# A two-layer graph network on one core: score weights loaded first by column halves, score products split in two sums

## The chip, the cores and the metric

The kernel runs on one NeuronCore of one Trainium2 chip. The metric is the device time of one execution in microseconds (us). A core has five engines with instruction queues of their own: TensorE (PE; its weight loads are listed as PEld), VectorE (DVE), ScalarE (ACT), GpSimd (POOL) and SyncE (SP), which here only issues DMAs. ACT and POOL issue DMAs too. All DMAs share 16 DMA engines.

## The reference

128 graphs of 128 nodes with 512 features pass through two layers, all in float32.

```python
# layer 0
h = maximum(layernorm(x), 0)
Xw = h @ Wv + bv;  sj = Xw @ aw[:512];  si = Xw @ aw[512:]
e = leaky_relu(sj[:, None, :] + si[:, :, None] + ab, 0.2)
T = adj * exp(e);  T = T / (sum(T, -1) + 1e-12)
H = h @ Wk[0] + (T @ h) @ Wk[1] + (T @ T @ h) @ Wk[2] + biases
x = x + relu(H)
# layer 1
h = maximum(layernorm(x), 0)
q, k = split(h @ Wqk);  v = h @ Wv1
w = mask * sum(q * (adj @ (k * mask)), -1) / sqrt(512)
x = x + softmax(w over nodes) * v
```

Two rearrangements matter here. Layer 0 needs from Wv only two columns, Wv times each half of `aw`; they are put beside Wk[2], so one product gives h @ Wk[2] and both attention terms. Layer 1 needs from Wqk only the 512 x 512 matrix Wq Wk^T, the score matrix: q . (adj k) = h Wq Wk^T (adj h)^T. It is computed once, from Wqk transposed.

## The kernel before, in words

**Pairs.** Layer 0 takes the graphs in 64 pairs p (`G` = 2). Each 512 x 512 product of a pair is one level of Strassen (`strassen`): seven products in the order 1, 5, 6, 2, 7, 3, 4 on four PSUM banks, the partial sums moved between the banks by ACT copies. `y2(p)` is h @ Wk[2] with the two attention columns, on the banks of set2 (a2, b2, c2, e2). `y10(p)` is h @ Wk[1] and h @ Wk[0] side by side, on set1 (a1, b1, c1, e1), into which `seed_a` and `seed_e` first copy the biases. Left operands are the transposed h and four sums of its blocks (`left_sums`). Right operands are blocks of the weights and four differences of them (`combine`): `right2` for y2, `right10` for y10. `attention(p)` makes T from the two columns, the adjacency and an exponential. For that, `spread_columns` transposes the column over the partitions; for pairs 0 and 1 this is done on TensorE in the middle of y10(0)'s first product or behind y2(1). `inner` and `outer` apply T, and `norm2` makes h for layer 1, which follows from about 1300 us on with its own loop.

**Before pair 0's y2** stands the set-up, which the change rewrites. All line numbers are those of the kernel before.
- Loads (lines 144 to 190). SP issues x of pair 0, wqk in four chunks of 128 rows (`wqk_sb`, named tl in the profile), x of pair 1, and then the weights of layer 0 by `rows` (170 to 174): wv0 (t), Wk[2] (w) and Wk[1], Wk[0] (r). `rows` permutes the rows so that chunk c goes to partitions 32c to 32c + 31, four rows to each. The chunks 0 and 1 go on SP, 2 and 3 on POOL, there behind a one-element copy (`gate`, L178) that reads wqk's third chunk.
- `weights_transposed(c)` transposes chunk c of wqk on TensorE in groups of four, and ACT and VectorE copy them out of PSUM into `wqt` and `wkt`. Filling products on ones (`warm`, `warm_whole`) stand between the chunks.
- `score_matrix(f)` (L316 to L323) then makes 128 rows of the score matrix with four accumulated products on a bank of set1; ACT copies it to `rl`.
- Pair 0's h is normalised from `statistics` and transposed on TensorE (`transposed_by_pe`); later pairs go by a store to DRAM and four reloads in blocks (`by_blocks`: hd, hv), which VectorE transposes (`transposed`, in `begin`).
- `attention_columns` (L252 to L262) makes the two columns Wv aw on VectorE: eight products of 128 x 512 with a sum each (L258), and two small copies into the weights of y2 (w).
- `constant_columns` and `attention_constant` give the constant bv . aw + ab, which a small TensorE product in y2(0), behind its seventh product, adds up over the partitions; VectorE copies it to `cz`.

**What sets the order.** A scheduler orders each engine's instructions by its own estimate of when each will be ready. `tc.issue_after(x)` forbids it to put an instruction before x on its engine. `ordered` (L88 to L91) chains all TensorE work in the order of the program. `behind(what, op)` (L83 to L86) puts an operation behind the latest one recorded under a name: "wk" and "wq" for the set-up's copies on VectorE and ACT, "u" for the attention columns, "u2", "s7" for copies inside a Strassen product, "rs" and "aggr" for statistics, "right" for weight differences, "lrelu" and "t" for the attention. These helpers record all their operations at one line, so in the profile most TensorE work is L91, and many copies are L86: tiles tell them apart. A DMA queue takes its issues in program order, each also waiting until the DMA that used its semaphore eight issues earlier has landed.

## Time and profile before

| | |
|---|---|
| Time, median of 3 runs | 2207.72 us (2206.92 to 2208.58) |
| The profiled execution's own time | 2207.71 us |
| Its span, first to last instruction | 2205.9 us |
| TensorE busy | 2197.3 us of it |
| First score product | at 13.19 us |
| First product of y2(0) | at 28.27 us |
| First product of y2(1) | at 49.37 us |

Times of the profile count from the start of the span. A row of the timeline gives start, duration, engine, line, operation, output tile <- input tiles, shape and count, and in brackets how long the engine stood idle before it, and what ended this. A float32 product is two instructions in the profile, whose modelled ends overlap those that follow, so distances are taken from start to start. In the chain of waits each row is a start, a duration and what the chain was in: an engine's work, a DMA under way, or "issue", for which the profile shows no cause.

### The profile page before, as it was taken

The page shows a single profiled execution, that of the slowest core. Times are in us where ns is not written, and L with a number is a line of the kernel's source. Part 1 is how long each engine was busy: PE and PEld are TensorE (multiplying, and loading weights), DVE is VectorE, ACT ScalarE, POOL GpSimd, SP SyncE. Part 2 cuts the span into 40 slices and gives each one's busy share as a digit, 9 for nine tenths or more (in the row PEclk, how much of TensorE's full clock was granted, in tenths as well). Part 3 has the DMA queues.
Part 4 walks back from the last instruction along what each step waited for, and adds up shares of the span by engine and source line. Part 5 has one row for each costly group of instructions (what it writes and reads, how often), then busy time and mean ns, then how long its engine had stood idle before and what let it go on. Part 6 is the DMA issues. An engine that isn't in the chain of part 4 may idle for free.

```text
span 2205.9 us, 29564 instructions
## 1 busy us (share of the span) xinstructions
PE 2197.3 (100%) x8127; PEld 1536.1 (70%) x8127; DVE 1699.8 (77%) x4544; ACT 1233.0 (56%) x2854; POOL 782.6 (35%) x957
## 2 busy tenths in 40 slices
PE   9999999999999999999999999999999999999998
PEld 6666666665666666566666666688788878887886
DVE  6778788777878877777877777588777777777777
ACT  4555555555555455555545554456666666666665
POOL 3222222222222222222222222255545554555454
PEclk9999999999999999999999999999999999999999
DMA  7788788887878888887878887867888788787877
GB/s 212 204 226 241 221 237 241 234 245 226 247 223 244 234 239 234 225 245 225 243 222 239 232 232 207 285 180 220 234 226 228 214 236 224 231 212 230 233 212 182
DMA packets 431874, 503.14 MB, mean 228 GB/s; under 512 B 102113, under 2 KB 280289, under 8 KB 427741
## 3 DMA queue, kind: packets, MB, share of 16 engines
q1 hardware_dynamic: 379544, 374.67, 56.1%
q0 software_dynamic: 51744, 126.05, 23.2%
q8 instruction: 65, 1.06, 0.2%
q14 instruction: 101, 0.82, 0.1%
q10 hardware_dynamic: 420, 0.54, 0.1%
HBM read 287.17 MB, written 213.94 MB: 227 GB/s over the span
## 4 chain that ended last, share of the span: by engine, by line
PE 98%; DMA 1%; DVE 1%; issue 0%; SPq 0%; DVEq 0%; POOL 0%
PE a L91 29%; PE c L91 26%; PE b L91 26%; PE e L91 17%; DMA t<-in_L_gnn_Wv_dram 0%; DMA tl<-in_L_gnn_Wqk_dram 0%; DVE junk L258 0%; DVE c L720 0%; DVE h L720 0%; DVE junk L720 0%; SPq L146 0%; DVEq L1429 0%; DVE x L389 0%; PE a L194 0%; SPq L101 0%
## 5 line engine op out<-in xcount | busy, mean ns | idle before, releaser
L720 POOL TENSOR_TENSOR c<-s,c 128x512 f32<-128x512 f32 (+1 forms) x186 | 201.2, 1095 | 252.3 <-DVE s L720 247.2
L475 POOL DMA_DIRECT2D fd<-fw x124 | 78.8, 639 | 492.8 <-DVE fw L463 458.5
L111 POOL DMA_DIRECT2D agb<-in_adj_dram x256 | 149.9, 592 | 260.2 <-DVE aT L86 235.5
L91 PE MATMUL a<-r,x 128*128 128x512 f32 x512 | 240.7, 592 | 0.0
L91 PE MATMUL b<-rw,in 128*128 128x256 f32 x884 | 212.0, 379 | 0.0
L91 PEld LDWEIGHTS b<-rw,in 128*128 128x128 f32 x884 | 168.0, 190 | 23.3 <-issue 0.5
L91 PEld LDWEIGHTS a<-r,x 128*128 128x128 f32 x512 | 97.1, 190 | 95.0 <-issue 91.3
L86 ACT COPY s<-c 128x257 f32<-128x257 f32 (+1 forms) x128 | 61.6, 481 | 171.4 <-PE c L91 171.4
L86 ACT COPY b<-a 128x257 f32<-128x257 f32 (+1 forms) x128 | 59.4, 464 | 167.7 <-PE a L91 165.2
L720 POOL TENSOR_TENSOR c<-c 128x1024 f32<-128x1024 f32 x61 | 144.2, 2363 | 10.9 <-DVE c L720 10.4
L91 PE MATMUL a<-w,x 128*128 128x257 f32 x512 | 132.0, 380 | 1.2 <-DVE w L86 1.1
L91 PE MATMUL b<-w,sx 128*128 128x257 f32 x512 | 132.1, 380 | 0.1
L463 DVE STREAM_TRANSPOSE fw<-hv 128x256 f32<-128x256 f32 x248 | 88.3, 414 | 52.1 <-DMA hv<-h2d 51.7
L91 PE MATMUL c<-t,sx 128*128 128x512 f32 x256 | 120.3, 592 | 0.0
L91 PE MATMUL e<-t,sx 128*128 128x512 f32 x256 | 120.3, 592 | 0.0
L91 PE MATMUL c<-t,x 128*128 128x512 f32 x256 | 120.3, 592 | 0.0
L91 PE MATMUL b<-t,sx 128*128 128x512 f32 x256 | 120.3, 592 | 0.0
L91 PE MATMUL b<-r,sx 128*128 128x512 f32 x256 | 120.3, 592 | 0.0
L720 DVE SCALAR_TENSOR_TENSOR junk<-agg,wscale,c 128x512 f32<-128x512 f32 x126 | 96.2, 763 | 30.0 <-POOL c L720 24.8
L720 ACT ACTIVATE c<-c,wcol 128x512 f32<-128x512 f32 x124 | 86.3, 720 | 55.7 <-DVE wcol L720 55.7
L86 ACT COPY c<-b 128x257 f32<-128x257 f32 (+1 forms) x128 | 59.4, 464 | 98.9 <-PE b L91 98.9
L91 PEld LDWEIGHTS a<-w,x 128*128 128x128 f32 x512 | 97.1, 190 | 15.9 <-DVE w L86 1.9
(282 smaller groups left out, 5318.3 us busy)
## 6 DMA issues: line engine op xcount, KB each, us to landing
fd<-fw POOLq DMA_DIRECT2D x93, 512.0 KB, 4.8
xg<-in_x_dram SPq DMA_DIRECT2D x64, 512.0 KB, 7.0
x1d<-x SPq DMA_DIRECT2D x64, 512.0 KB, 5.6
h2d<-h SPq DMA_DIRECT2D x64, 512.0 KB, 3.0
hd<-h SPq DMA_DIRECT2D x63, 512.0 KB, 3.1
hv<-hd SPq DMA_DIRECT2D x252, 128.0 KB, 3.9
hv<-h2d SPq DMA_DIRECT2D x248, 128.0 KB, 4.4
h<-h2d SPq DMA_DIRECT2D x62, 512.0 KB, 7.7
```

Of the source, the lines that this page charges most:

```text
L86: return op(*args, **how)
L91: done["mm"] = op(*args, **how).ins
L111: nc.gpsimd.dma_start(agb[p][c * S32:(c + 1) * S32].rearrange("p g q i -> p (g q) i"), v[c])
L463: done["c12"] = nc.vector.transpose(blocks[:, k, j].rearrange("p f (n b) -> p f n b", n=Q), hv[:, j].rearrange("p n (k f a) -> p k f n a", ...
L475: done["fd"] = nc.gpsimd.dma_start(FD[q].rearrange("p o j k n -> p o (j k n)")[:, slots], FW[0].rearrange("p o j k n -> p o (j k n)")[:, s ...
L720: done[engine] = op(*args, **how).ins
```

## The change

- wqk is loaded first, before x of pair 0, in eight DMAs: by column halves (`oh`: the first or second 256 columns of Wq and of Wk at once), and in each by 128-row chunks. Each partition gets two pieces of 1 KB.
- `rows` splits by f in place of c: each DMA fills all 128 partitions with one row of 2 KB each.
- wv0 and Wk[2] are loaded wholly on SP, x of pair 1 between the two; the gate of POOL's loads reads the last of wv0, and POOL keeps half of Wk[1] and Wk[0]. The adjacency loads of pairs 0 and 1 stand behind these.
- The transposes run by quarters (`ch`, `oh`), and each score product is two sums: over the first 256 columns of Wq and Wk, then over the rest, added to the same bank. The program alternates transposes and score products, and pair 0's transposes stand between score products too.
- Of the filling products, one small one and two whole banks stay, all at the start.
- VectorE: pair 0's statistics stand behind the first transposed copies; pair 1's statistics and normalisation move from before y2(0) into it; two of the four differences of `right10` run beside y2(0), one behind `lrelu`, one behind `t`; the left sums come behind the attention columns. Both copies of pair 0's transposes are on ACT.

The diff, cut to its core:

```diff
+    for oh in range(2):
+        for ch in range(2):
+            part = [bass.AP(tensor=wqk.tensor, offset=wqk.offset + (ch * HC + c) * P * 2 * D + oh * HD,
+                            ap=[[2 * D, P], [D, 2], [1, HD]]) for c in range(HC)]
+            for c in range(HC):
+                nc.sync.dma_start(wqk_sb[:, ch * HC + c].rearrange("p (a o) -> p a o", a=2)[:, :, oh * HD:(oh + 1) * HD],
+                                  part[c])
     load_x(0)
-    for c in range(DC):
-        nc.sync.dma_start(wqk_sb[:, c], wqk[c * P:(c + 1) * P])
-    load_x(1)
...
-        for c in chunks:
-            queue.dma_start(dst[c * S32:(c + 1) * S32],
-                              w[c * P:(c + 1) * P].rearrange("(f a) o -> a f o", a=S32))
+        for f in chunks:
+            queue.dma_start(dst[:, f], bass.AP(tensor=w.tensor, offset=w.offset + f * S32 * D,
+                                               ap=[[P * D, DC], [D, S32], [1, D]]))
...
-    done["gate"] = nc.gpsimd.tensor_copy(gate, wqk_sb[:, 2, :1]).ins
+    for dst, w in weights0[:2]:
+        rows(dst, w)
+        if dst is wv0_sb:
+            load_x(1)
+    done["gate"] = nc.gpsimd.tensor_copy(gate, wv0_sb[:, DC - 1, :1]).ins
...
+    def weights_transposed(ch, oh, banks):
+
+        for a, bank in enumerate(banks):
+            pt = bank.rearrange("p (k n) -> p k n", n=P)
+            for c in range(HC):
+                for o in range(HC):
+                    at = a * D + (oh * HC + o) * P
+                    ordered(nc.tensor.transpose, pt[:, o * HC + c if a else c * HC + o, :],
+                            wqk_sb[:, ch * HC + c, at:at + P], ident)
...
-    def score_matrix(f):
+    def score_matrix(f, oh):
         bank = set1[f]
-        for o in range(DC):
+        for o in range(oh * HC, (oh + 1) * HC):
             ordered(nc.tensor.matmul, bank, wqt[:, o, f].rearrange("p c a -> p (c a)"), wkt[:, o],
-                    start=(o == 0), stop=(o == DC - 1))
+                    start=(o == 0), stop=(o == DC - 1), skip_group_check=True)
...
-            (nc.vector.tensor_copy if j else nc.scalar.copy)(dst[:, j], pt)
+            nc.scalar.copy(dst[:, j], pt)
...
+    warm(1, e2)
+    warm_whole(b2)
+    warm_whole(c2)
+    done["warm"] = done["wk"] = done["wq"] = done["mm"]
+    weights_transposed(0, 0, (a2, e2))
+    weights_transposed(1, 0, (c1, e1))
+    attention_vector_columns()
+    attention_vector(0)
+    weights_transposed(0, 1, (a2, e2))
+    attention_vector(1)
+    score_matrix(0, 0)
+    masks()
+    score_matrix(1, 0)
+    h0_rs = behind("wk", statistics, xg[0], "wq")
+    behind("aggr", bias_columns)
+    weights_transposed(1, 1, (a2, e2))
+    score_matrix(2, 0)
+    score_matrix(3, 0)
+    h0 = behind("wq", norm_relu, xg[0], True, h0_rs)
+    done["wq"] = done["h"]
+    score_matrix(0, 1)
     hT0 = lefts.tile([P, G, DC, N], FP, name="x")
+    transposed_by_pe(h0, hT0, (a2, e2))
+    behind("wk", behind, "rs", attention_columns)
+    LEFT[0] = behind("u", left_sums, hT0)
+    for f in range(1, Q):
+        score_matrix(f, 1)
     for p in range(2):
+        behind("loads", load_adj, p)
     with tc.issue_after(done["u"]):
         right2 = combine(halves(r2, W2), [t2[:, i] for i in range(4)])
+    def beside_y2():
+        RS0[1] = behind("right", statistics, xg[1], "u2")
+        bias()
+        constant_columns()
+    right10_steps = combine_steps(halves(r10, HD), pairs(t10))
+    right10 = combined(halves(r10, HD), pairs(t10))
+    with tc.issue_after(done["m"]):
+        y2(0, {2: beside_y2, 7: attention_constant})
+        with tc.issue_after(done["right"]), tc.issue_after(done["rs"]):
+            for step in right10_steps[:2]:
+                step()
+        behind("u2", seed_a)
+        behind("s7", norm0, 1, RS0.pop(1))
+        behind("s7", seed_e)
         spread_columns(0)
         attention(0)
+        behind("lrelu", right10_steps[2])
+        behind("t", right10_steps[3])
```

More of the change, by code (lines that the diff above doesn't have):

```diff
@@ L170, in rows @@
     def rows(dst, w, chunks=range(DC), queue=nc.sync):
-        for c in chunks:
-            queue.dma_start(dst[c * S32:(c + 1) * S32],
-                              w[c * P:(c + 1) * P].rearrange("(f a) o -> a f o", a=S32))
+        for f in chunks:
+            queue.dma_start(dst[:, f], bass.AP(tensor=w.tensor, offset=w.offset + f * S32 * D,
+                                               ap=[[P * D, DC], [D, S32], [1, D]]))
     gate = setup.tile([P, 1], FP, name="gate")
-    done["gate"] = nc.gpsimd.tensor_copy(gate, wqk_sb[:, 2, :1]).ins
     weights0 = [(wv0_sb, wv0), (r2[:, :, 1:1 + D], wk[2])] + [(r10[:, :, k], wk[1 - k]) for k in range(2)]
+    for dst, w in weights0[:2]:
[3 more added lines that the diff above has]
+    done["gate"] = nc.gpsimd.tensor_copy(gate, wv0_sb[:, DC - 1, :1]).ins
     with tc.issue_after(done["gate"]):
-        for dst, w in weights0[:2]:
+        for dst, w in weights0[2:]:
             rows(dst, w, range(HC, DC), nc.gpsimd)
@@ L184 @@
         nc.gpsimd.dma_start(awc, aw.rearrange("(a p c) o -> p a (c o)", a=2, c=DC))
-        nc.gpsimd.dma_start(ab_bc, bcast(ab, 0, 1))
-        for dst, w in weights0[2:]:
-            rows(dst, w, range(HC, DC), nc.gpsimd)
-    for dst, w in weights0:
+        done["loads"] = nc.gpsimd.dma_start(ab_bc, bcast(ab, 0, 1)).ins
+    for dst, w in weights0[2:]:
         rows(dst, w, range(HC))
@@ L298, in bias @@
         for i, to in enumerate((bias_a, bias_e)):
-            behind("wk", over_partitions, to[:, 1], bkt[:, 0, i * n:(i + 1) * n], n)
-    def weights_transposed(chunks):
-        banks = [a2, e2, a1, b1, c1, e1]
-        for c in chunks:
-            for a in range(2):
-                bank = banks[(c * 2 + a) % len(banks)]
-                pt = bank.rearrange("p (o i) -> p o i", o=DC)
-                for o in range(DC):
-                    at = a * D + o * P
-                    ordered(nc.tensor.transpose, pt[:, o, :], wqk_sb[:, c, at:at + P], ident)
-                if a:
-                    done["wk"] = behind("wq" if c == HC else "wk", nc.scalar.copy if c == HC else nc.vector.tensor_copy, wkt[:, :, c * P:(c + 1) * P], pt).ins
-                else:
-                    done["wq"] = behind("wq", nc.scalar.copy, wqt[:, :, :, c, :], pt.rearrange("p o (f a) -> p o f a", f=Q)).ins
@@ L316, in score_matrix @@
-    def score_matrix(f):
+            behind("aggr", over_partitions, to[:, 1], bkt[:, 0, i * n:(i + 1) * n], n)
+    def weights_transposed(ch, oh, banks):
[6 more added lines that the diff above has]
+                            wqk_sb[:, ch * HC + c, at:at + P], ident)
+            if a:
+                on = "wq" if oh > ch else "wk"
+                done[on] = behind(on, nc.scalar.copy if oh > ch else nc.vector.tensor_copy,
+                                    wkt[:, oh * HC:(oh + 1) * HC, ch * HD:(ch + 1) * HD],
+                                    bank.rearrange("p (o n) -> p o n", o=HC)).ins
+            else:
+                done["wq"] = behind("wq", nc.scalar.copy,
+                                    wqt[:, oh * HC:(oh + 1) * HC].rearrange("p o f c a -> p (o f) c a")[
+                                        :, :, ch * HC:(ch + 1) * HC],
+                                    bank.rearrange("p (c o a) -> p o c a", c=HC, a=S32)).ins
@@ L318, in score_matrix @@
+    def score_matrix(f, oh):
         bank = set1[f]
-        for o in range(DC):
+        for o in range(oh * HC, (oh + 1) * HC):
             ordered(nc.tensor.matmul, bank, wqt[:, o, f].rearrange("p c a -> p (c a)"), wkt[:, o],
-                    start=(o == 0), stop=(o == DC - 1))
+                    start=(o == 0), stop=(o == DC - 1), skip_group_check=True)
         done["m"] = done["mm"]
-        nc.scalar.copy(rl[:, f, 0], bank)
+        if oh:
+            done["wq"] = behind("wq", nc.scalar.copy, rl[:, f, 0], bank).ins
@@ L759, in inner_sums @@
                 lambda: dve(nc.vector.tensor_sub, s[:, 3], b[0, 1], s[:, 1])]
-    warm(7, e2)
+    warm(1, e2)
     warm_whole(b2)
-    done["warm"] = done["mm"]
-    h0_rs = statistics(xg[0])
-    done["wk"], done["wq"] = done["rs"], done["ln"]
-    weights_transposed(range(1))
+    warm_whole(c2)
[5 more added lines that the diff above has]
+    weights_transposed(0, 1, (a2, e2))
@@ L768 @@
+    attention_vector(1)
[7 more added lines that the diff above has]
+    score_matrix(3, 0)
     h0 = behind("wq", norm_relu, xg[0], True, h0_rs)
     done["wq"] = done["h"]
-    attention_vector_columns()
-    attention_vector(0)
-    warm_whole(c2)
-    weights_transposed(range(1, 2))
-    attention_vector(1)
-    bias_columns()
@@ L776 @@
-    warm(2, b2, False)
-    weights_transposed(range(2, 3))
-    warm(2, b2, False)
-    weights_transposed(range(3, 4))
-    hT0 = lefts.tile([P, G, DC, N], FP, name="x")
-    transposed_by_pe(h0, hT0, (a1, b1))
-    masks()
-    bias()
-    rs1 = behind("wk", statistics, xg[1], "wq")
-    LEFT[0] = left_sums(hT0)
-    behind("left", attention_columns)
+    score_matrix(0, 1)
+    hT0 = lefts.tile([P, G, DC, N], FP, name="x")
+    transposed_by_pe(h0, hT0, (a2, e2))
+    behind("wk", behind, "rs", attention_columns)
@@ L787 @@
+    LEFT[0] = behind("u", left_sums, hT0)
+    for f in range(1, Q):
+        score_matrix(f, 1)
     for p in range(2):
-        load_adj(p)
-    for f in range(Q):
-        score_matrix(f)
-    behind("wq", norm0, 1, rs1)
+        behind("loads", load_adj, p)
     with tc.issue_after(done["u"]):
         right2 = combine(halves(r2, W2), [t2[:, i] for i in range(4)])
-    constant_columns()
-    with tc.issue_after(done["right"]):
-        right10 = combine(halves(r10, HD), pairs(t10))
-    with tc.issue_after(done["right"]), tc.issue_after(done["m"]):
-        y2(0, {7: attention_constant})
-        seed_a()
-        seed_e()
+    RS0 = {}
@@ L805 @@
         load_adj(2)
-    RS0 = {}
     for p in range(NP):
```

## The prediction

> **What bounds the kernel now.** I read the busy shares first, then the chain of work that ended last, then the first 60 us engine by engine, because every line of the change except one (the later use of `rows`) sits there.

> ```profile
> PE 2197.3 (100%) x8127; PEld 1536.1 (70%) x8127; DVE 1699.8 (77%) x4544; ACT 1233.0 (56%) x2854; POOL 782.6 (35%) x957
> ...
> PE 98%; DMA 1%; DVE 1%; issue 0%; SPq 0%; DVEq 0%; POOL 0%
> ```

> TensorE is idle for 8.6 us of a span of 2205.9, and its clock row is full. From 60 to 2100 us the table by stretches has it busy without a gap. So nothing that the change does to other engines can pay there; what it can pay is the time at which the steady stream begins. That stream begins with pair 0's `y2`. The chain of the first 30 us says what it waits for:

> ```profile
> 2.21 7.36 DMA tl<-in_L_gnn_Wqk_dram
> ...
> 9.75 9.44 DMA t<-in_L_gnn_Wv_dram
> 19.19 3.00 issue
> 22.19 0.70 DVE junk L258 x2
> ...
> 28.03 0.22 DVE w L86 x2
> ...
> 28.27 1.13 PE a L91 x4
> ```

> The second half of `wv0` is issued on POOL only behind the gate (9.63), its landing lets VectorE start the eight products of `attention_columns` (L258) at 22.19, and these end in the column that y2(0) needs at 28.27. TensorE's own rows beside it:

> ```profile
> 4.25 1.92 PE L229 MATMUL b<-ones 128*128 128x512 f32 x2
> 5.98 1.08 PE L91 MATMUL a<-ident,tl 128*128 128x128 f32 x4
> ...
> 8.34 0.65 PE L91 MATMUL a<-ident,tl 128*128 128x128 f32 x4
> ...
> 13.19 3.70 PE L91 MATMUL a<-wkt,wqt 128*128 128x512 f32 x8
> ...
> 23.60 3.60 PE L91 MATMUL e<-wkt,wqt 128*128 128x512 f32 x8
> 28.27 1.13 PE L91 MATMUL a<-w,x 128*128 128x257 f32 x4 [1.08 <-DVE w L86]
> ...
> 35.18 0.27 PE L194 MATMUL a<-ident,y 128*128 128x128 f32 x1
> ...
> 36.15 0.27 PE L194 MATMUL a<-ident,y 128*128 128x128 f32 x1
> ```

> The wait on VectorE is only 1.08 us. Without it y2(0) could not start before 27.2, since the score products (13.19 to about 27.1, back to back) fill the time. **So the two chains are nearly equal, and a gain has to shorten both**: TensorE's through an earlier start of the score products, the other through an earlier `wv0`.

> [...]

> ```profile
> GB/s 0 0 52 363 333 370 405 322 345 285 344 410 412 380 393 167 147 186 210 194 205 197 218 292 333 249 328 273 317 273 236 243 309 300 257 273 317 223 201 281
> ```

> With 128-partition loads 322 to 412; from the 16th slice (11.3 us), when the 32-partition `rows` loads run, 147 to 218. I go by the trace. [...] In the trace four transposes take 0.89 us at 5.98 (start to next start) and 0.49 at 8.34, so the clock rose near 7. I go by these rows. The new kernel's warm-up (one product on e2, two whole banks) ends at 1.10 + 0.45 + 2 x 1.73 = 5.0, as late as the first weights arrive.

> **The change, part by part.**

> *Loads of wqk.* Four DMAs of 4 KB rows become eight of 1 KB pieces, ahead of x0. The packet records give medians of 159, 84 and 46 ns for 4096, 2048 and 1024 bytes, so 16 engines move 412, 390 and 356 GB/s: a 256 KB piece takes 16 x 46 = 0.74 us. Eight SP issues at about 0.5 us (four took 2.09) keep up. x0 came first before and landed at 4.60 (its statistics start there); its 256 packets of 2 KB take 1.34 us, so I set a landing at 3.26 plus the packets ahead. The second to fourth wqk chunks came about 1.2 us later than this gives: 8.3 (TensorE's wait), 9.6 (POOL's gate) and 10.9 (issue 2.7 plus 8.2 to landing) for 7.1, 8.4 and 9.7. POOL's small loads of `nm` and `bkj` run then, and run now, so I carry this 1.2 from 6 us on. Pieces then land at 4.0, 4.7, 5.5, 7.4 (first column half), 8.1, 8.9, 9.6, 10.3 (second). TensorE does its first eight transposes from 5.0 at the slow clock, the next eight by about 8.2, and ends the third group at 8.9 + 6 x 0.11 + 0.05 = **9.6**. Copies of the first half (0.59 ACT, 0.69 VectorE) are ready by 9.0, so the score products start there, against 13.19.

> *TensorE from there.* 16 products of 0.86 (13.75; the sum in two halves adds none), eight more transposes (0.87), pair 0's eight (0.87), `nm` (0.11): 15.6. **y2(0) at 25.2, 3.1 earlier than 28.27.** The three fill-in warmings (1.9 us) go, but they lay in gaps.

> *Whether the other chain allows it.* x0 lands at 11.7, later than 4.60, and its statistics now stand ahead on VectorE: bn 1.5, bias columns 0.8, ACT 0.6, five small steps 0.9: 15.0; wkt copy 15.7. `wv0` on 128 partitions lands at 14.4 (four x 0.67). Products L258: 8 x 0.735 = 5.9, columns 0.3: 21.9. Left sums and right2 run alternately after it (first of each by 23.1). y2's first product needs the columns at 25.2, its second the sums at 26.2: **3 us of cover**. If the cover goes, each us is paid on TensorE. h0 on ACT is ready at 16.6; its transposes come at 19.2. `wk2` shares the engines with POOL's four r10 loads, whose gate moves from 9.63 to 14.4, and lands by 22 at worst (1 MB each at half of 390 GB/s from 16.5). POOL drops four issues (1.18 + 1.09 us); pair 0's adj blocks behind it need to be there only for aT at Y+9.7, 34.9, and were issued by 28 before.

> *y2(0) and y10(0).* y2 itself keeps its 6.9 us. The four r10 differences (1.2 each) ran before its end at 37.15; now two stand before the attention chain, one behind lrelu, one behind t. With Y the start of y2: r10's first two end by Y+8.7 (needed Y+9.3 and Y+11.0), t at Y+12.6 (its transposes come at Y+14.4), the last two by Y+13.8 (needed Y+14.7 and Y+18.1). No wait. But pair 1's norm is now behind y2's seventh-product copy: its last statistics step stands behind `cz` on VectorE, which waits for the constant product (Y+5.3). Then on ACT: two normalisations 1.52, seed_e 0.5, and only then the copy of y10's column (0.38), ready about Y+8.2. The second spread transpose could run at Y+7.9 (36.15 before): **0.4 lost, bounds 0 to 0.6** (none if the norm finds its scale 0.4 earlier; 0.6 if ACT's copies do not overlap).

> *Pair 1's reload.* Its store moves from 26.02 to Y+7.4 = 32.6, and lands in about 3 (it took 9 before, behind the weights). Four reloads of 0.45, landing 3 to 4 later: Y+15. VectorE takes them up after y10's two additions, the second bound to product 3 (Y+18.9, done 19.4): transposes 20.7, first sum 21.1. y2(1) starts at Y+21.9. Covered by 1.2 us. x3 and adj loads behind it on SP keep over 3 us. `wv1` on 128 partitions (passes 1 to 4): no wait for it existed, nothing.

> **Sum.** -3.1 + 0.4 = -2.7, against the profiled execution's own 2207.71 (2205.9 span, 1.8 around it); the median of runs, 2207.72, is the same. **2205.0.** Bounds: without the 1.2 of late landing and without the 0.4, y2(0) begins near 24.0 (first landing rule alone, 7.7 + 0.7 + 15.6): 2203.4. Faster pieces would add little: TensorE's 24 transposes alone, eight at 0.22 and sixteen at 0.11 from 5.0, end at 8.5.

> **Rivals.**
> 1. *Landings without delay:* 2203.4. For it: the delay is seen in one execution, at one place. Against: the same POOL loads still run then. Chance 0.22 (2202.8 to 2204.2).
> 2. *The clock rises late.* Fill-ins are gone, and transposes now wait singly for pieces. [...] Against: TensorE is without a gap from 1.1 to 7. The same time comes if VectorE's 3 us of cover are overdrawn by 1.7. Chance 0.16 (2206 to 2207.7).
> 3. *Slower: the split pieces are served like the 32-partition loads.* At 190 GB/s the 3.67 MB up to the end of wv0 need 19.3 us: landed 22.6, L258 done 28.5, y2(0) at 28.9, with the 0.4: 2208.7. It decides once L258 starts after 22.0. Against: 1024-byte packets took 46 ns and all partitions are written. Chance 0.10, its tail going to 2213.
> The forecast itself (2204.2 to 2206): 0.52. That the change does not do what it says is excluded: the order of instructions shows the products split, and the rest of the kernel the same but for a few swaps.

> About 0.2% (4.4 us) is what can be told from no change. Below 2203.3 lies a part of rival 1: faster 0.13; slower 0.04; same 0.83. The range 2202.8 to 2208.0 leaves out a little of rivals 1 and 3.

> **What would show it.** First score product at 9.6, y2(0) at 25.2 with no VectorE wait before it, GB/s above 300 from 3 to 20 us, the second spread transpose 0.4 late, no new gap before y2(1). Wrong if L258 starts after 19, if transposes past 8 us take over 0.2 us each, or if y2(1) waits for pair 1's reload.

## The result, and the profile after

| | before | after |
|---|---|---|
| Time, median | 2207.51 us | **2228.75 us** (2228.08 to 2230.03) |
| Ratio to before, 95% interval | | **1.0096** [1.0079, 1.0114] |
| Span of the profiled execution | 2205.9 us | 2226.8 us |
| First score product | 13.19 us | 10.40 us |
| First product of y2(0) | 28.27 us | 39.62 us |
| First product of y2(1) | 49.37 us | 70.38 us |
| Span behind y2(1) | 2156.5 us | 2156.4 us |

The change made the kernel 21 us slower, where 2.7 us of gain were forecast. All of it is lost before pair 1's y2: that moved by 21.0 us, the span by 20.9. From the page of the changed kernel (line numbers are now its own: `rows` is L177, the attention columns are L264, the weight differences L205):

```profile
PE 2199.5 (99%) x8107; PEld 1533.9 (69%) x8107; DVE 1692.0 (76%) x4543; ACT 1233.6 (55%) x2855; POOL 780.4 (35%) x953
...
PE 97%; SPq 2%; DMA 1%; DVE 0%; issue 0%; DVEq 0%
```

TensorE has nearly the same work, but the chain that ended last now holds 2% of "SPq", SP's own queue, some 40 us in which the issue of loads was the path. Before it was 0%. TensorE's waits, in total over the run (engine, line, what it waited for: us, times, longest):

```profile
PE a L91 <- DVE w L86: 15.5, 2, 13.5
PE a L91 <- DMA r<-in_L_gnn_Wk_dram: 2.4, 2, 2.0
PE c L91 <- DMA tl<-in_L_gnn_Wqk_dram: 1.3, 2, 1.0
```

And the same on TensorE's timeline:

```profile
10.40 1.88 PE L91 MATMUL a<-wkt,wqt 128*128 128x512 f32 x4
...
24.29 1.88 PE L91 MATMUL e<-wkt,wqt 128*128 128x512 f32 x4
39.62 1.20 PE L91 MATMUL a<-w,x 128*128 128x257 f32 x2 [13.46 <-DVE w L86]
42.87 1.23 PE L91 MATMUL a<-w,x 128*128 128x257 f32 x2 [2.05 <-DVE w L86]
43.93 2.08 PE L91 MATMUL e<-w,sx 128*128 128x257 f32 x4
...
55.16 1.10 PE L91 MATMUL a<-r,x 128*128 128x512 f32 x2 [2.00 <-DMA r<-in_L_gnn_Wk_dram]
56.43 3.58 PE L91 MATMUL e<-t,sx 128*128 128x512 f32 x4 [0.17 <-DVE t L205]
...
70.38 1.03 PE L91 MATMUL a<-w,x 128*128 128x257 f32 x4
```

The score products begin nearly when forecast and end at 26.0. Then TensorE stands for 13.46 us and again for 2.05 us before y2(0), and behind each long wait some rows run at half speed (2.08 us for four products that otherwise take 1.03, 3.58 for four that take 1.88; the granted clock is 0.50 from 29 to 46 us and from 56.3 to 59.6, and 1.00 between). The wait is put down to VectorE's copy into w; VectorE's timeline says what that copy waited for:

```profile
16.20 0.68 DVE L264 SCALAR_TENSOR_TENSOR junk<-t,aw_bc 128x512 f32<-128x512 f32 x1
...
18.57 0.69 DVE L264 SCALAR_TENSOR_TENSOR junk<-t,aw_bc 128x512 f32<-128x512 f32 x1 [0.95 <-DMA t<-in_L_gnn_Wv_dram]
...
21.17 0.69 DVE L264 SCALAR_TENSOR_TENSOR junk<-t,aw_bc 128x512 f32<-128x512 f32 x1 [1.17 <-DMA t<-in_L_gnn_Wv_dram]
...
23.78 0.69 DVE L264 SCALAR_TENSOR_TENSOR junk<-t,aw_bc 128x512 f32<-128x512 f32 x1 [1.18 <-DMA t<-in_L_gnn_Wv_dram]
...
24.51 0.69 DVE L264 SCALAR_TENSOR_TENSOR junk<-t,aw_bc 128x512 f32<-128x512 f32 x1
39.26 0.26 DVE L86 COPY w<-ucol 128x4 f32<-128x4 f32 x1 [14.05 <-DMA w<-in_L_gnn_Wk_dram]
42.64 0.17 DVE L86 COPY w<-ucol 128x4 f32<-128x4 f32 x1 [3.12 <-DMA w<-in_L_gnn_Wk_dram]
```

The pieces of wv0 come in steps of 2.60 us: 256 KB in 2.6 us are 101 GB/s. The attention columns are made at the pace at which the pieces land, the last one at 23.7 (forecast 14.4). Their last product ends at 25.2, still before the score products end at 26.0, so the late wv0 alone did not hold TensorE. What held it is Wk[2], into which the columns are copied: its loads stand behind those of wv0 on SP, and the two copies waited for it until 39.3 and 42.6 (forecast 22 at worst). The DMA rows of the changed kernel from 13 to 22 us, in 40 slices of 0.225 us (busy share of the 16 engines in tenths, and the rate):

```profile
DMA  2222222295599999934322222222222222222222
GB/s 100 91 100 100 100 100 100 100 191 146 164 346 355 391 355 255 237 73 91 91 73 100 109 91 100 100 109 100 91 100 109 100 82 109 109 100 91 100 109 100
```

The same stretch of the kernel before:

```profile
DMA  9898999989999899899999999989698997989999
GB/s 164 164 255 173 246 182 182 237 173 209 200 173 255 164 200 264 164 191 228 291 328 255 319 291 328 364 246 364 191 410 246 319 319 218 328 246 346 364 255 337
```

These two rows are to be read together. Before, the first half of the row has about 200 GB/s at a busy share of 9 tenths: all engines worked, each slowly. After, 100 GB/s come with a share of 2 tenths: **few engines work at all**, and those at full speed. In the middle of the row, near 15 us, x of pair 1 comes: issued behind wv0 on the same queue, plain rows over the same 128 partitions. It doesn't wait for wv0 to end (23.7), and while it runs, share and rate are full (9, 346 to 391 GB/s). So neither the queue nor the chip is slow; the new form of `rows` leaves engines idle, and another load can use them. The packet records agree: a 2048-byte packet of these loads took about 170 ns before and takes 84 after, and 4 x 2048 bytes in 84 ns are 98 GB/s. The same records give how many packets of 1 KB or more were under way at once: after, from 18 to 23 us, four in 81% of the time and five in nearly all the rest; before, from 11.3 to 16 us, 15 at the least and mostly 16 or 17. The records do not name the engine, but four engines of 16 fit all these numbers.

### The profile page after: what moved, and what is told of

Same layout as the page of the kernel before. It is cut to its first block, busy times and chain, and to the rows that moved or that the text cites. A ratio compares the mean times of both kernels' runs of the same rounds, so it can differ in the third digit from the quotient of the medians.

```text
span 2226.8 us, 29543 instructions
## 1 busy us (share of the span) xinstructions
PE 2199.5 (99%) x8107; PEld 1533.9 (69%) x8107; DVE 1692.0 (76%) x4543; ACT 1233.6 (55%) x2855; POOL 780.4 (35%) x953
## 3 DMA queue, kind: packets, MB, share of 16 engines
q8 instruction: 65, 1.06, 0.2%
## 4 chain that ended last, share of the span: by engine, by line
PE 97%; SPq 2%; DMA 1%; DVE 0%; issue 0%; DVEq 0%
PE a L91 28%; PE c L91 26%; PE b L91 26%; PE e L91 17%; SPq L177 1%; DMA r<-in_L_gnn_Wk_dram 1%; SPq L149 0%; DVE c L732 0%; SPq L101 0%; DVE h L732 0%; DVE t L205 0%; DVE junk L732 0%; DVEq L1451 0%; DVE x L401 0%; DVE z L86 0%
## 5 line engine op out<-in xcount | busy, mean ns | idle before, releaser
L91 PE MATMUL a<-r,x 128*128 128x512 f32 x512 | 240.9, 592 | 2.4 <-DMA r<-in_L_gnn_Wk_dram 2.4
L91 PE MATMUL b<-rw,in 128*128 128x256 f32 x884 | 212.0, 379 | 0.0
L91 PEld LDWEIGHTS b<-rw,in 128*128 128x128 f32 x884 | 168.0, 190 | 23.3 <-issue 0.5
L91 PEld LDWEIGHTS a<-r,x 128*128 128x128 f32 x512 | 97.1, 190 | 97.8 <-issue 94.2
L86 ACT COPY b<-a 128x257 f32<-128x257 f32 (+1 forms) x128 | 59.4, 464 | 186.5 <-PE a L91 184.0
L86 ACT COPY s<-c 128x257 f32<-128x257 f32 (+1 forms) x128 | 61.6, 481 | 169.3 <-PE c L91 169.3
L91 PE MATMUL a<-w,x 128*128 128x257 f32 x512 | 133.3, 382 | 15.7 <-DVE w L86 15.5
L732 POOL TENSOR_TENSOR c<-c 128x1024 f32<-128x1024 f32 x61 | 144.2, 2364 | 11.2 <-DVE c L732 10.8
L91 PE MATMUL b<-w,sx 128*128 128x257 f32 x512 | 132.1, 380 | 0.0
L91 PE MATMUL e<-t,sx 128*128 128x512 f32 x256 | 122.0, 599 | 0.2 <-DVE t L205 0.2
L91 PE MATMUL c<-t,sx 128*128 128x512 f32 x256 | 120.3, 592 | 0.0
L91 PE MATMUL b<-t,sx 128*128 128x512 f32 x256 | 120.3, 592 | 0.0
L91 PE MATMUL c<-t,x 128*128 128x512 f32 x256 | 120.3, 592 | 0.0
L91 PE MATMUL b<-r,sx 128*128 128x512 f32 x256 | 120.3, 592 | 0.0
L91 PEld LDWEIGHTS a<-w,x 128*128 128x128 f32 x512 | 97.4, 191 | 31.0 <-issue 14.3
L86 ACT COPY c<-b 128x257 f32<-128x257 f32 (+1 forms) x128 | 59.4, 464 | 99.3 <-PE b L91 99.2
```

The source lines that it names most:

```text
L86: return op(*args, **how)
L91: done["mm"] = op(*args, **how).ins
L732: done[engine] = op(*args, **how).ins
```

## The experiments

All ratios are against the kernel before, run on the same chip (medians there 2207.2 to 2207.7). The first columns are from the profiled execution. Executions of one kernel lie some 2 to 5 us apart (2205.8 to 2209.2 for before), and the profiled one need not be the median: that of e1 (2216.44) and that of e4 (2228.41) were the slowest of theirs.

| kernel | y2(0) starts | y2(1) starts | median us | ratio [95%] |
|---|---|---|---|---|
| before | 28.27 | 49.37 | 2207.51 | 1 |
| after | 39.62 | 70.38 | 2228.75 | 1.0096 [1.0079, 1.0114] |
| e1: after, old `rows` | 29.08 | 58.20 | 2213.95 | 1.0029 [1.0017, 1.0040] |
| e2: after, plain rows | 25.80 | 46.58 | 2205.38 | 0.9991 [0.9984, 0.9997] |
| e3: after, 8 in front | 29.33 | 56.70 | 2215.25 | 1.0032 [1.0021, 1.0043] |
| e4: before, new `rows` | 37.86 | 68.79 | 2226.28 | 1.0085 [1.0072, 1.0099] |
| e5: after, 16 in front | 27.43 | 50.20 | 2207.97 | 1.0003 [0.9995, 1.0011] |
| e6: before, plain rows | 27.18 | 48.04 | 2206.68 | 0.9998 [0.9990, 1.0006] |
| e7: e1 on two queues | 27.95 | 52.52 | 2210.04 | 1.0012 [1.0005, 1.0018] |
| e8: e7, wqk on two queues | 29.29 | 53.69 | 2212.36 | 1.0024 [1.0015, 1.0032] |
| e9: e1, constants first | 26.24 | 52.35 | 2211.13 | 1.0017 [1.0010, 1.0024] |
| e10: e9, all in order of need | 26.14 | 53.66 | 2212.87 | 1.0026 [1.0016, 1.0036] |
| e11: e10, earlier second gate | 25.81 | 49.41 | 2208.58 | 1.0007 [1.0000, 1.0014] |

From y2(1) to the end every one of them takes 2156.2 to 2156.5 us, e4 2157.5. So the start of y2(1) can stand for the time.

**e4: the kernel before with nothing but the new `rows`.**

```diff
-        for c in chunks:
-            queue.dma_start(dst[c * S32:(c + 1) * S32],
-                              w[c * P:(c + 1) * P].rearrange("(f a) o -> a f o", a=S32))
+        for f in chunks:
+            queue.dma_start(dst[:, f], bass.AP(tensor=w.tensor, offset=w.offset + f * S32 * D,
+                                               ap=[[P * D, DC], [D, S32], [1, D]]))
```

> The kernel before, with only the loads of rows in the new form (front dimension 4). Theory A: each DMA of 256 KB takes 2.6 us. SP's eight need 21 us from 11.5 on, POOL's eight the same or share the four engines with them: if POOL's run on other engines, wv0 is there at 17 and Wk[1], Wk[0] at 32 to 35, time 2208 to 2216; if both queues share four engines, all sixteen need 42 us, wv0 is there at 22 to 25, Wk[2] near 33, r10 near 53, and the time is 2222 to 2232. Theories B and C: 2207.5, as before.

Measured: 2226.28. TensorE's timeline:

```profile
37.86 2.08 PE L91 MATMUL a<-w,x 128*128 128x257 f32 x4 [10.85 <-DVE w L86]
```

This single edit gives 18.6 of the 21.2 us, with the queues, the gate and the whole order of before. B and C are not needed for the bulk. The time is the one expected if both queues share four engines (2222 to 2232), but the trace does not bear out that reason. Its DMA row from 11 to 30 us (0.475 us a slice):

```profile
DMA  7748595979989799869554437545433222222363
```

Up to about 22 us, where SP and POOL load at the same time, the share is mostly 5 to 9 tenths, and 8 packets at the least were under way. So POOL's loads used more engines than SP's four. All the same the stretch moved 117 GB/s in the mean: SP's packets of 2048 bytes took 194 to 227 ns (medians) beside POOL's, and 84 to 89 where SP loads alone. Why the packets are slower beside another queue is not shown.

**e2: the changed kernel, each load reading 128 consecutive rows.** The weights' rows then stand in another order than the products expect, so e2 shows what the loads cost and is no replacement; the same holds for e3, e5 and e6.

```diff
-            queue.dma_start(dst[:, f], bass.AP(tensor=w.tensor, offset=w.offset + f * S32 * D,
-                                               ap=[[P * D, DC], [D, S32], [1, D]]))
+            queue.dma_start(dst[:, f], w[f * P:(f + 1) * P])
```

> The changed kernel, with each DMA of rows reading 128 consecutive rows of 2 KB into 128 partitions. The weights' rows so stand in another order than the kernel needs, so the product with them is another one; sizes, partitions, packets of 2 KB, number of DMAs and queues are those of the changed kernel. Theory A: 128 in front on both sides, 16 engines, 330 to 390 GB/s; wv0 is there by 15.5, Wk[2] by 20, VectorE no longer holds TensorE, y2(0) begins where the score products ended in the changed kernel, 26.0, and with 0.4 lost at the second spread transpose the time is 2205.8 (2205 to 2207). Theories B and C, and a fourth (writes to 128 partitions in 2 KB pieces are slow as such): 2220 or more.

Measured: 2205.38, within 0.4 of both the expectation and the original forecast. The same destination, bytes, number of packets and place in the queue; only the DRAM side's front dimension went from 4 to 128. Its DMA rows of 13 to 22 us:

```profile
DMA  9999999999999999999999999999999999999989
GB/s 337 410 428 337 401 419 346 400 410 346 410 410 346 401 410 355 401 382 373 410 364 392 401 364 401 410 364 464 401 355 382 382 355 428 391 364 392 428 328 410
```

Four times the rate of after at four times the share, with the same packet time (87 against 84 ns). The order of the rows in DRAM changes with it; e3 and e5 below, which keep it broken, show that the count in front is what matters for the number of engines. This is theory A, and it leaves C with no loss. TensorE's timeline:

```profile
10.20 1.88 PE L91 MATMUL a<-wkt,wqt 128*128 128x512 f32 x4
...
25.80 1.03 PE L91 MATMUL a<-w,x 128*128 128x257 f32 x4
...
32.32 0.27 PE L199 MATMUL a<-ident,y 128*128 128x128 f32 x1
...
33.30 0.32 PE L199 MATMUL a<-ident,y 128*128 128x128 f32 x1
...
46.58 1.03 PE L91 MATMUL a<-w,x 128*128 128x257 f32 x4
```

**e6: the kernel before with plain rows** (the same edit in its `rows`; other products, as in e2).

> The kernel before, with only the loads of rows as 128 consecutive rows to 128 partitions (row order not the kernel's, so other products). It asks what full-rate loads alone are worth to the old order of the work. Theory A with TensorE's score products as the second chain: wv0 comes before 17, the VectorE wait of 1.08 us before y2(0) goes, y2(0) at 27.1 in place of 28.27, and right10's operands come earlier: 2206.6 (2206.0 to 2207.3). The rest of the 2.3 us that the plain rows gained on the changed kernel then belongs to the earlier score products. If the gain came from the loads alone: 2205.4.

Measured: 2206.68 (expected 2206.6); y2(0) follows the score products without a wait on VectorE:

```profile
27.18 1.03 PE L91 MATMUL a<-w,x 128*128 128x257 f32 x4
```

By y2(1), faster loads alone are worth 1.3 us (49.37 to 48.04), and the rest of the change with fast loads another 1.5 (to e2's 46.58). By the medians it is 0.9, with an interval that includes no change, and 1.3. So the rewritten order gains once the loads are fast, and both chains had indeed to be shortened, as the prediction read it.

**e3 and e5: the front dimension set to 8 and to 16.** The line of e3 (e5 has 16 in place of 8):

```diff
+                                               ap=[[DC * (P // 8) * D, 8], [D, P // 8], [1, D]]))
```

> As the plain rows, but the DRAM side is 8 blocks of 16 rows (64 rows apart), so its front dimension is 8 (row order again not the kernel's, so other products). Theory A: 8 engines, 195 GB/s while such a DMA runs alone, DMA busy share 0.5; wv0 takes 5.4 us and is there at 18, Wk[2] by 25 to 28 (POOL's loads share the engines), r10 by 33; y2(0) at 26.5 to 29, time 2206 to 2211. If it is the broken row order in DRAM that is slow rather than the engine count: near the changed kernel's 98 GB/s and 2228.

> As the run with eight in front, but the DRAM side is 16 blocks of 8 rows (32 rows apart): the broken row order stays, the front dimension is 16 (row order not the kernel's, so other products). Theory A (engines used = the front dimension, up to 16): 16 engines, the same as the plain rows, 2205.4 (2204.5 to 2206.5), over 350 GB/s from 11 to 22 us. If the breaks in the row order cost: between the plain rows and eight in front, 2208 to 2213.

DMA rows of e3 from 13 to 22 us:

```profile
DMA  9998645544554555545555464455555546999876
GB/s 228 273 200 209 146 118 182 200 182 182 218 200 182 191 218 209 200 182 209 209 182 137 109 137 164 164 218 200 200 191 127 164 173 210 246 218 246 218 228 264
```

And of e5:

```profile
DMA  9999999999999999999999999998999999999999
GB/s 228 264 282 273 273 273 273 291 264 291 255 291 228 291 273 255 273 291 291 337 291 264 246 219 264 173 219 200 282 273 246 300 228 282 264 282 264 255 264 246
```

With 8: share 4 to 5 where SP's loads run alone, about 190 GB/s, packets 84 to 94 ns, 8 or 9 of them under way in 93% of the time from 18 to 20 us: eight engines. The rate was as expected, the time above it (2215.25 for 2206 to 2211): Wk[2] was there only at 29.1 and 32.9. From 22 to 29 us, with POOL's loads of Wk[1] beside it, 16 packets and more were mostly under way, so POOL's ran on other engines too, and yet SP's took 192 ns (median).

With 16: all engines busy, but 264 GB/s and not 388, since a packet takes 128 ns in place of 87. The count of engines is right, and the packet time is a second term. In the old form (32 partitions, all engines) packets take about 170 ns. That is twice 84; the cause is not shown. Whether the 128 ns of e5 come from its shorter runs of rows in DRAM (the other expectation for it), or from something else, is not shown either.

The time of e5 does not tell of the loads alone. Its y2(0) comes 1.6 us later than e2's without any wait before it, because the score products began later:

```profile
11.78 1.93 PE L91 MATMUL a<-wkt,wqt 128*128 128x512 f32 x4
```

In this execution TensorE waited 1.27 us for a piece of wqk, and the last twelve transposes ahead of the first score product took 0.21 us each in place of 0.11. The small product of the constant waited 1.28 us more.

| form of the load | front | packets under way | packet ns | GB/s |
|---|---|---|---|---|
| new `rows` | 4 | 4 to 5 | 84 | 98 to 100 |
| e3 | 8 | 8 to 9 | 84 to 94 | 179 to 207 |
| e5 | 16 | 16 to 18 | 128 | 262 to 270 |
| e2, plain rows | 128 | 16 to 18 | 87 | 384 to 389 |
| old `rows`, 32 partitions | 32 | 16 to 18 | about 170 | about 200 |

So in these five forms the packets under way are as many as the DRAM side has in front, or one more, where that is 4 or 8, and 16 to 18 where it is 16, 32 or 128. That bears out theory A for the forms measured.

**e1: the changed kernel with the old `rows`.**

> The changed kernel, with only the loads of rows put back: one DMA per 128-row chunk into 32 partitions, four rows of 2 KB to each. All other moves of the change stay, wv0 and Wk[2] wholly on SP too. Theory A (the new form runs on 4 of the 16 DMA engines, because the pattern on the DRAM side begins with a dimension of 4; that alone cost the 21 us): the old form has 32 in front on both sides and uses 16 engines at the 150 to 218 GB/s of the kernel before, so wv0 needs 5.5 us in place of 10.7 and is there at 18, Wk[2] at 25 to 26, y2(0) begins at 26 to 27.5, and the time is 2206 to 2209. Theory B (the loss comes from carrying all of wv0 and Wk[2] on SP's queue, without POOL's half): still over 2220. Theory C (it comes from splitting the score products or from the new VectorE order): no change, 2228.

Measured: 2213.95, in none of the expected ranges (2206 to 2209 for A, over 2220 for B). The old form takes back 14.8 of 21 us (14.8 = 2228.75 - 2213.95), and 6.3 stay against before (2207.69 beside it). TensorE's waits in the first 62 us of the profiled execution:

```profile
PE c L91 <- DVE r L353: 3.1, 1, 3.1
PE c L91 <- DMA tl<-in_L_gnn_Wqk_dram: 1.9, 1, 1.9
PE a L91 <- DVE w L86: 1.4, 1, 1.4
```

This speaks for B as a second, smaller part: at 200 GB/s everything that stands behind the loads is late by a little. The 3.1 us lie in y2(0) before the small product of the constant: `awc`, which it needs, is now issued behind Wk[1] on POOL and landed late (VectorE stood 2.34 us for it); the eight products behind it ran at half speed (1.86 and 1.92 us for four in place of 1.03). e7 to e11 try to repair this with the reference's own row order.

**e7 and e8: loads on two queues.** e7 gives POOL half of wv0 and Wk[2] again, with its gate on the last piece of wqk, the constants ahead of Wk[1], and the attention behind the weight differences. e8 also puts half of wqk on ACT's queue.

```diff
-        rows(dst, w)
+        rows(dst, w, range(HC))
-    done["gate"] = nc.gpsimd.tensor_copy(gate, wv0_sb[:, DC - 1, :1]).ins
+    done["gate"] = nc.gpsimd.tensor_copy(gate, wqk_sb[:, DC - 1, D - 1:D]).ins
```

> A version for use: the changed kernel with the loads of rows in 128-row chunks of 32 partitions, as before, and wv0 and Wk[2] halved between SP (chunks 0, 1) and POOL (chunks 2, 3) again, so that both halves of the partitions are written at once; POOL's gate reads the last piece of wqk, the small constants come before Wk[1] and Wk[0] on POOL, and pair 0's attention is held behind the first two differences of right10. Theory A: 250 to 330 GB/s from 11 us on as in the kernel before, wv0 there by 18, Wk[2] by 24, y2(0) at 26 to 27: 2205.5 to 2207. If the two queues do not overlap: y2(0) at 29 as with one queue, 2210 or more.

> The version with two queues, and wqk's eight pieces issued from SP and ACT by turns of two, since one SP issue of two pieces per row took 0.65 us. If the issue rate holds back the first pieces: the third group of transposes ends 0.5 to 0.8 earlier, y2(0) too, time 0.5 to 0.8 under the version with two queues. If the engines hold them back: the same time.

e7 lies at 2210.04, where it was expected if the queues do not overlap, though y2(0) came at 27.95 and not at 29. e8 missed both of its forecasts. In e7 POOL's half of wv0 was there only at 21.9, as before (22.2), though issued from 10.8 on: the first packets moved at 141 to 231 GB/s. y2(0) came at 27.95 behind 2.31 us of waiting, and two of its rows ran at half speed (1.92 us each in place of 1.03). In e8 the two halves of wqk arrived interleaved, so the first was complete later: the second transposes stood 1.89 us, the 20 behind them took 0.21 us each in place of 0.11, and the first score product began at 12.37 in place of 9.88. That product's row takes 2.38 us in e8 and the next 1.88; in e7 four transposes take 0.60 from 6.33 on (1.06 in e8), and the first score product 1.88.

**e9, e10, e11: one queue, in order of need.** e9 is e1 with the three small loads of the constant ahead of Wk[1] on POOL. e10 has these loads behind a gate on wqk's last piece, Wk[1] and Wk[0] behind a second gate on Wk[2], x of pair 1 behind Wk[2], the attention behind the differences, pair 1's normalisation behind y10's first copy. e11 moves e10's second gate to wv0.

```diff
     with tc.issue_after(done["gate"]):
         nc.gpsimd.dma_start(bvc, bv0.rearrange("(p c) -> p c", c=DC))
         nc.gpsimd.dma_start(awc, aw.rearrange("(a p c) o -> p a (c o)", a=2, c=DC))
         nc.gpsimd.dma_start(ab_bc, bcast(ab, 0, 1))
-        done["gate"] = nc.gpsimd.tensor_copy(gate, r2[:, 0, D:D + 1]).ins
+        done["gate"] = nc.gpsimd.tensor_copy(gate, wv0_sb[:, DC - 1, :1]).ins
```

> The changed kernel with the old form of the row loads (as in e1), and with one more edit: POOL issues its three small loads for the constant (bvc, awc, ab_bc) ahead of its four loads of Wk[1] and Wk[0], in place of behind them. In e1 the constant product stood 3.08 us for VectorE, which stood for awc, and the eight rows behind it ran at the slow clock (1.6 us more). Theory (e1's loss behind y2(0)'s start is this one landing): the gap goes with the clock fall, the remaining waits stay (1.4 before y2(0), 0.7 to 1.9 ahead): 2208 to 2210. Rival (the loads as a whole are too late, and the wait only moves to the differences of right10, whose loads now start later): 2211 to 2214, with the waits of TensorE on the tiles of r and t in place of the constant.

> The changed kernel with the old form of the row loads, set up so that Wk[2] and the constants come before everything else: POOL's small loads for the constant behind a gate on the last piece of Wqk, its loads of Wk[1] and Wk[0] behind a second gate on Wk[2]; x of pair 1 behind Wk[2] on SP; the attention of pair 0 behind the differences of right10, the normalisation of pair 1 behind y10's first copy. If what was left of e1's loss is the shared queues and the order in which ACT and VectorE take up their work: y2(0) at 26 to 26.5 without the constant's wait, 2205.5 to 2207. If the 32-partition form (about 200 GB/s) is itself the limit, or the later loads of Wk[1] now hold up y10(0): 2208 to 2211.

> The kernel of e10 with its second gate on the last piece of wv0 (18.5 us there) in place of Wk[2] (23.7): POOL's two chunks of Wk[1] and of Wk[0] start 5 us earlier. In e10 y2(0) began at 26.14 without a wait, and then TensorE stood 3.96 us before y10(0) for those chunks, and four rows more ran at half clock. If only the late gate held e10 up: y2(0) at 26.1 to 26.7, y10(0) at 35 without a long gap, 2205 to 2206.5. If the 32-partition form at about 205 GB/s is the limit: wv0, Wk[2], Wk[1], Wk[0] and x of pair 1 are 4.7 MB behind 11.3 us, all landed by about 34.5, y10(0) at 35.5 to 36.5 with 1 to 2.5 us of waits spread over y2(0) and y10(0): 2207 to 2209.

e9: 2211.13, in the range of its rival (2211 to 2214). The constant's wait fell from 3.1 to 0.6, and the one before y10(0)'s second product, on the weight differences, grew from 0.69 to 1.66. In the profiled executions y2(1) gained 5.9 us (58.20 to 52.35), 2.8 of them by y2(0)'s start and 3.0 behind it, but by the medians e9 gains only 2.8 on e1. In e1's profiled execution TensorE had waited 1.9 us for a piece of wqk, which this edit does not touch. e10, at 2212.87, lies above both of its ranges: y2(0) at 26.14 without a wait, and the loss one step later:

```profile
26.14 1.03 PE L91 MATMUL a<-w,x 128*128 128x257 f32 x4
...
37.83 3.62 PE L91 MATMUL a<-r,x 128*128 128x512 f32 x4 [3.96 <-DMA r<-in_L_gnn_Wk_dram]
```

e11 lies at 2208.58, in the second of its ranges (2207 to 2209). Wk[2] and Wk[1] are there in time (0.2 us of waiting for Wk[1]), and y2(0) starts at 25.81, as with the fast loads of e2:

```profile
25.81 1.03 PE L91 MATMUL a<-w,x 128*128 128x257 f32 x4
...
33.52 1.95 PE L91 MATMUL a<-r,x 128*128 128x512 f32 x4 [0.20 <-DMA r<-in_L_gnn_Wk_dram]
35.31 1.88 PE L91 MATMUL e<-t,sx 128*128 128x512 f32 x4
38.77 1.98 PE L91 MATMUL b<-t,sx 128*128 128x512 f32 x4 [1.59 <-ACT b L86]
...
49.41 1.03 PE L91 MATMUL a<-w,x 128*128 128x257 f32 x4
```

and yet y2(1) begins at 49.41, where before has 49.37. What 2.46 us of earlier start brought is given back in y10(0): 1.59 us before its third product, 0.36 before the second spread transpose, 0.20 for Wk[1]; the remaining third of a microsecond is no single wait. ACT shows the largest of them:

```profile
37.19 0.42 ACT L86 ACTIVATE z<-z 128x256 f32<-128x256 f32 x1 [2.84 <-DVE z L86]
37.55 0.69 ACT L86 ACTIVATE aT<-aT,maskT 128x128 f32<-128x128 f32 x2
38.15 0.58 ACT L86 COPY b<-a 128x512 f32<-128x512 f32 x1
```

The copy from a to b, for which the product waits, stands behind the attention's exponential and mask, and these wait for VectorE's differences, which wait for Wk[1] (33.5). That the attention stands behind the differences is an edit of e7, e8, e10 and e11; e11 without it was not run. The rate of the old form stays what it was, its lateness only moved to the next consumer. The median, 2208.58, is above before's by 0.07%, with an interval that just touches no change; the profiled execution (2207.65) was among the faster ones. A kernel with the reference's products that beats the one before was not found. A load that keeps the needed row order, has 16 or more in front on the DRAM side and has packets of 84 to 87 ns was not tried.

## Why the prediction was wrong, point by point

- *The bound and the stage* were read rightly: time follows the start of y2(1) in all thirteen kernels, and e6 and e2 show that both chains had to shorten.
- *Loads of wqk.* First score product at 10.40 for 9.6. SP took 5.45 us for eight issues, 0.68 each and not "about 0.5", and from 3 to 9.75 us 209 to 348 GB/s moved, less than the 356 taken; the third group's transposes waited for a piece until 9.69, and x0's statistics began at 12.55 for 11.7. Which of the two made the pieces late is not shown. An error of 0.8.
- *TensorE from there*: 15.6 us forecast; 10.40 to the end of the last score product at 26.0 is 15.6.
- **The step that failed**: "`wv0` on 128 partitions lands at 14.4 (four x 0.67)", and after it "lands by 22 at worst (1 MB each at half of 390 GB/s from 16.5)". Both took the rate from the packet time (84 ns) times 16 engines. The packet time was right (84 ns measured) and the engines were four. At 98 GB/s wv0 came at 23.7, and Wk[2] behind it, slowed further by POOL's loads, at 42.6. The "3 us of cover" still bore the late wv0 (columns done at 25.2, score products at 26.0); the late Wk[2] overdrew it by 13.46 and 2.05 us on TensorE. The sum has no term for Wk[2] because 22 lay before 25.2.
- *The sign of being wrong*, "if L258 starts after 19", did not appear: L258 started at 16.20, on the first piece of wv0. It watched the wrong load. "GB/s above 300 from 3 to 20 us" did fail, from 12 us on most plainly (98).
- *Rival 3* had the direction and the resource, loads that land late. Its point, "It decides once L258 starts after 22.0", was not reached (16.20; the last pair of these products began at 23.78). And it set the rate at 190 GB/s for a wrong reason (the split pieces of wqk, during which 209 to 348 GB/s moved), and dismissed the rest with "1024-byte packets took 46 ns and all partitions are written". Packet time and partitions did not tell how many engines get packets: on 128 partitions, with packets of 84 ns in the changed kernel and 87 in e2, 4 to 5 were under way in the one and 16 to 18 in the other. Its 2208.7 stays 20 us short.
- *Rival 2*, the clock at half speed while transposes wait singly for pieces, whose cost no trace had shown, did not come in the profiled execution of the changed kernel; it came in those of e5 and e8, where the transposes took 0.21 us each and the first score product began at 11.78 and 12.37. In the changed kernel the clock is full from 5.1 to 28.9 us, and the slow one (0.50) comes later, from 29 us on in the wait of 13.46 and from 56.3 behind that of 2.00. The table by stretches of the changed kernel (stretch, length, busy time of PE, PEld, DVE, ACT, POOL with instructions, then clock, DMA share, GB/s):

```profile
24.00:39.00 15.00, 2.17 (x6) 0.62 (x4) 1.18 (x4) 1.17 (x2) 6.20 (x11) 0.67 0.58 134
39.00:52.00 13.00, 9.61 (x34) 6.80 (x34) 7.33 (x27) 4.35 (x11) 2.86 (x5) 0.73 0.48 145
52.00:60.00 8.00, 5.83 (x10) 2.32 (x11) 4.82 (x9) 1.87 (x6) 0.08 (x1) 0.79 0.36 128
```

  From y2(0) to y2(1) the changed kernel takes 30.76 us, e2 20.78. Of the 10.0 between, 4.9 are waits (2.05, 0.28, 0.44, 2.00, 0.17), and the other 5 are mostly rows at the slow clock (granted: 0.73 from 39 to 52 us, 0.79 from 52 to 60). The whole: 13.8 by the later start than e2, 10.0 of this, and 2.8 that e2 gains on before: 13.8 + 10.0 - 2.8 = 21.0.
- *y10(0)'s 0.4 loss* did not come where loads are fast: the spread transposes of e2 are 0.98 apart (0.97 before). ACT had y10's column in time. In e7, with VectorE and ACT late, the same place cost 1.15. That e2 meets the forecast is partly luck, since errors cancelled: its first product of y2(0) is 0.6 later than forecast, its spread 0.4 better, and from y2(0) to y2(1) it is another 0.3 faster than before (20.78 for 21.10), which nobody forecast; y2(1) came 2.8 earlier where 2.7 were forecast.
- *Pair 1's reload* made no gap in e2, as forecast.

With the engine count in the sum, the working would have found it: 1 MB of wv0 at 98 GB/s takes 10.7 us, and Wk[2] another 10.7: 23.7 + 10.7 = 34.4 as an estimate, and it came some 8 us later (42.6), with the loads of POOL beside it.

## What to carry to other kernels

Cost a DMA as engines times bytes per packet over packet time, take both the packet time and the count of packets under way from a trace of the same form, and not the count from the partitions it fills: rewriting a load to "all 128 partitions" made it half as fast here (98 GB/s for about 200), because its DRAM side began with a 4 (8 in front gave about 190 GB/s, 16 gave 264, 128 gave 388). In these profiles, about 200 GB/s with a busy share of 9 went with slow packets (about 170 ns, before), and 100 GB/s with a share of 2 with few engines (4 to 5 packets of 84 ns under way, after). And a stage that feeds a nearly full TensorE has as many deadlines as it has loads: getting the first one earlier pays only if each later one moves too, as e10 and e11 show.

## What the runs showed of the hardware

- Loads of two queues with four in front do not simply add up. In the changed kernel SP alone moved 98 GB/s with packets of 84 ns and 4 to 5 under way; from 27 to 31 us, with POOL's loads beside it, 9 to 17 were under way, but SP fell to 56 GB/s and its packets rose to 158 ns (median). More engines worked, each more slowly; the cause is not shown.
- All 16 engines busy are not the full rate: with 16 packets and more under way, one of 2048 bytes took 87 ns (e2), 128 (e5) or about 170 (old `rows`).
- SP's issue of a DMA took 0.68 us for pieces of two 1 KB runs per partition; later the four loads of Wk[2] held SP 10.1 us and the four of Wk[1] and Wk[0] 17.1. In the kernel before, SP stood 4.4 us in four waits at `rows` (L173) for chunks of wqk to land before it issued. The rows of the changed kernel:

```profile
14.25 10.10 SPq L177 DMA_DIRECT2D w<-in_L_gnn_Wk_dram  x4
24.40 17.08 SPq L177 DMA_DIRECT2D r<-in_L_gnn_Wk_dram  x4
```

- Splitting a load that is waited for over two queues made it later (e8): from 3 to 8 us the two queues moved 614 and 637 packets of 1 KB, so both halves progressed together, and TensorE got its second piece at 7.62, where e7 on one queue had it at 6.05.
